# Attention's input normalisation folded into its projection weights; GpSimd's share of a product 160 columns instead of 152; two steps reordered

## The chip, the core and the metric

The kernel runs on one core of one Trainium2 chip. Its time is the device time of one execution in microseconds, taken as the median over several runs. Five engines run at once, each in its own order: TensorE (PE in the profile, its weight loads PEld), VectorE (DVE), ScalarE (ACT), GpSimd (POOL), and SyncE (SP), which here only issues DMAs. They wait for each other through semaphores.

## What is computed

The input x is 8 samples × 512 channels × 2304 positions, in fp32. Two layers are added to it, one after the other, each behind a group norm over 32 groups (mean and variance per group and sample).

```python
x = x + L0(_gn(x), Wq, bq, Wkv, bkv)          # linear attention, 8 heads, causal
x = x + L1(_gn(x), in_proj_w, ...)             # four Mamba blocks in a row

# L0, per sample: q, k, v = three 512x512 projections of the normalised input plus biases
Q, K, V = elu(q) + 1, elu(k) + 1, v
out = causal(Q K^T) V / (Q . cumsum(K) + 1e-10)

# L1, per sample and quarter of 128 channels: u is the quarter plus the output of the one before
xp, z = split(u @ Wi.T); xs = silu(conv(xp)); dt, Bm, Cm = split(xs @ Wx.T)
delta = softplus(dt @ Wdt.T + b)
h[t] = exp(delta[t] * A) * h[t-1] + delta[t] * xs[t] * Bm[t]     # 256 channels x 16 states
y[t] = sum_states(h[t] * Cm[t]) + xs[t] * D;  out = (y * silu(z)) @ Wo.T
```

After each quarter a gated mix (a maximum of input and Mamba output, and two sigmoid weights of means) makes the quarter's output.

## The kernel before

**The Mamba scan is the backbone.** A sample's quarter is cut into 6 chunks of 384 positions. A chunk is a `Job`, and there are 192 of them (8 samples × 4 quarters × 6 chunks). Two `Stream`s alternate, one for even and one for odd samples, by blocks of six jobs; such a block of six is called a pass here. A job has 8 slots, one for each half of the 256 channels and each of four groups of states. In a slot, `slot(k)` emits in this order:

- VectorE: `product` of the next slot (L890, the first 384 − TAIL columns of B × dxr; it reads B from a PSUM copy made by ScalarE at L863), then four `scan`s (L910), each on 128 partitions × 384 positions.
- ScalarE: `decay` (L900), one exponential per scan into a PSUM bank that a scan frees again; at most DEPTH = 3 are ahead (5 in front of the silu and softplus blocks), as far as banks are free.
- GpSimd: `last_product` of the slot after the next (L879, the last TAIL columns of the same product), then `weigh` (L923, the scanned states × C).
- TensorE: `gather` (L937), the sum over states into the bank yp, two slots later.

Besides, at the end of a half `gated` (L949, yz = yp × silu(z)) runs on VectorE, then TensorE projects it (L955) and VectorE takes the maximum (L966, fg). `prepare` makes a job's operands ahead: convolution (L722), gate (L733), silu (L758 to L763), softplus (L793), dx on GpSimd (L834), and the broadcast loads of dr, dxr, B and C through DRAM. `pass_on` mixes a finished quarter into the next one's input: L678 and L684 on TensorE, fu (L682) on ScalarE, xo (L696) on GpSimd, with loads of xb, fu and xo.

**Attention runs beside it.** It has passes too: one (sample, quarter of the output channels o = 0 to 3), six chunks each. `chunk(m)` is a generator; each of its `yield at(j), n` names the half-slot at which its next step is due and how many PSUM banks it needs. Chunks of attention follow each other at 16 half-slots, the length of a job, and lead the Mamba pass that needs them by about 61 half-slots. The steps: project q, k, v (L300, weights `wq` of the pass, biases `bqkv_sb`), features (exp L312 and relu L313 on ScalarE, q L359 and k L367 on VectorE), running sum of k (kc, L373 and L375), v (L378), a kept row (L382), pr = q × kc (L386, VectorE), transposes (L393), denominators and states (L405 to L437), transposes of the broadcast reciprocals (L445), q scaled (L450, VectorE), scores (L457, L467), relu of the scores (L479, ScalarE, `sm`), output (L484 to L498), copy and store (L508), statistics for the second norm (L512).

**Its normalisation.** `statistics(b)` collects mean and variance of a sample's groups (L243, L253), `group_norm` makes `norm`: scale in `norm[:, 0]`, shift in `norm[:, 1]`. In the first pass of each sample (o = 0) a chunk loads x, GpSimd normalises it in place (L324, four instructions of 128 × 384), and the result is stored to DRAM; the other three passes load that stored copy (L275).

**What sets the order.** All engines' programs are written out by hand at build time. `beside(half)` is called twice per slot. It first steps those heads (chunks of attention) whose next step needs no bank, then goes once through the tasks (prepare, pass_on, statistics, finale) and after them the heads, in order, and steps whatever is due and finds its banks free. So a step that needs a bank is emitted behind all tasks of that half-slot, and a step that needs none ahead of them. PSUM: six banks in a list `spare`, taken and returned in the order of emission, so the step that returns a bank determines who waits for whom. DMAs are all issued on SP, in the order of emission; stores wait there at least two half-slots.

Of the kernel before, what the change touches and what calls it, by code (L numbers as in the profile page):

```python
# [9 lines left out]
F32 = mybir.dt.float32  # L10
BF16 = mybir.dt.bfloat16
AF = mybir.ActivationFunctionType
ALU = mybir.AluOpType
# [4 lines left out]
P = 128  # L18
# [1 line left out]
LC = 384  # L20
NI, NQ, NGR = 4, 4, 4
SLOTS = 8
TAIL = 152
BANKS = 6
DEPTH = 3
LEAD = 11
# [23 lines left out]
def attention_then_mamba_kernel(  # L50
# [12 lines left out]
    nc = tc.nc  # L63
    B, _, L = x.shape
    NS = 16
    NC = L // LC
# [30 lines left out]
    wqs = []  # L97
# [72 lines left out]
    def save(out, in_):  # L170
        stores.append((half_no[0], out, in_))
# [48 lines left out]

    norms, xns, x1s, done, ksums = {}, {}, {}, {}, {}

    def statistics(b):

        xv = x[b].rearrange("(t p) l -> p t l", p=P)
        stats = small.tile([P, 4, NC, 6], F32, tag="stats_a", name=f"stats_a{b}", bufs=2)
        if b == 0:

            xs = []

            def load(c):
                t = mpool.tile([P, 4, 1 + LC], F32, tag="u", name=f"xs_{c}", bufs=5)[:, :, 0:LC]
                nc.sync.dma_start(out=t, in_=xv[:, :, c * LC : (c + 1) * LC])
                xs.append(t)

            for c in range(5):
                load(c)
            load_projections()  # L240
            for c in range(NC):
                for ct in range(4):
                    nc.vector.bn_stats(stats[:, ct, c, :], xs[c][:, ct, :])  # L243
                if c == 0:
                    load(5)
                    fetch(0)
        else:
            when = begins[b] + b % 2
            for i in range(4 * NC):
                yield (when - 4, 1) if b > 1 else "1", 0  # L250
                xs = piece(b, i)
                yield (when, 1) if b > 1 else "1", 0
                nc.vector.bn_stats(stats[:, i // NC, i % NC, :], xs)  # L253
                when += PERIOD
        norms[b] = yield from group_norm(stats, 4, f"a{b}", 2)
# [9 lines left out]
    def fetch(m):  # L265

        if m == len(parts):
            return
        b, o, c = parts[m]
        if (o, c) == (0, 0):  # L270
            xns[b] = dpool.tile([512, L], F32, tag="xn", name=f"xn_{b}", bufs=B)
            x1s[b] = dpool.tile([512, L], F32, tag="x1", name=f"x1_{b}", bufs=B)
        xn = apool.tile([P, 4, LC], F32, tag="xn", name=f"xn_{b}_{o}_{c}", bufs=2)
        src = (x[b] if o == 0 else xns[b]).rearrange("(t p) l -> p t l", p=P)
        nc.sync.dma_start(out=xn, in_=src[:, :, c * LC : (c + 1) * LC])  # L275
        fetched[m] = xn

    read, passes = [0], {}

    def chunk(m):  # L280

# [9 lines left out]
        def at(j, gap=1):  # L291
            return times[m] + j, gap
# [4 lines left out]
        def project(j):  # L297
            ps = bank()[:, 0:LC]
            for kt in range(4):
                nc.tensor.matmul(  # L300
                    ps,
                    wqs[m // NC][:, kt, j * P : (j + 1) * P],
                    xn[:, kt, :],
                    start=(kt == 0),
                    stop=(kt == 3),
                )
            return ps, bqkv_sb[:, j * 4 + o : j * 4 + o + 1]

        def feature(ps, bias):

# [2 lines left out]
            nc.scalar.activation(ps, ps, AF.Relu, bias=bias)  # L313
            return ex

        if o == 0:
            yield at(-4), 0
            while b not in norms or m not in fetched:
                yield "1w", 0
            xn, norm = fetched.pop(m), norms[b]  # L320
            for ct in range(4):
                if ct:
                    yield at(ct - 4), 0
                nc.gpsimd.tensor_scalar(  # L324
                    xn[:, ct, :],
                    xn[:, ct, :],
                    norm[:, 0, ct : ct + 1],
                    norm[:, 1, ct : ct + 1],
                    ALU.mult,
                    ALU.add,  # L330
                )
            save(xns[b].rearrange("(t p) l -> p t l", p=P)[:, :, cols], xn)
        while read[0] < m - 1:
            yield "1w", 0
        yield at(0), 1
        if o:
            xn = fetched.pop(m)
        if c == 0:
            passes[b, o] = (
                small.tile([P, 4, 64], F32, tag="S", name=f"S_{b}_{o}", bufs=2),  # L340
# [98 lines left out]
        yield at(15), 0  # L439
        rdb = new("rdb", 1, (P, 2 * NT, 64))  # L440
        nc.scalar.copy(rdb, rd.unsqueeze(2).to_broadcast([P, 2 * NT, 64]))
        yield at(17), 1
        rb = bank()[:, 0:LC].rearrange("p (i t) -> p i t", i=NT)
        for i in range(NT):
            nc.tensor.transpose(  # L445
# [19 lines left out]
        for i in range(NT):  # L465
            for h, sc in zip(heads_of, scs):
# [5 lines left out]
                    stop=i == NT - 1,  # L472
                    skip_group_check=True,
                )
        yield at(20), 0
        sms = []
        for par, sc in enumerate(scs):
            sm = new(f"sm{par}", 1, (P, NT, T))
# [43 lines left out]
    class Stream:  # L522
# [55 lines left out]
        def pass_on(self):  # L578
# [78 lines left out]
            for c in range(NC):  # L657

                cols, icols = slice(c * LC, (c + 1) * LC), slice(3 + c * LC, 3 + (c + 1) * LC)
                if now is None:  # L660
                    first = 2 * self.jobs[self.block * NC + c].start
                    yield (first - 33, 1), 0
                    now = loads(c)
                    yield (first - 25, 1), 0 if old is None else 1
                else:
                    yield "1", 0 if old is None else 1
                fu, xb, xa = now
                now = None
                if not last:
                    normed = dict(bias=norm[:, 1, :], scale=norm[:, 0, :])  # L670
                if old is None:
                    nc.scalar.activation(xi[:, icols], xb, AF.Identity, **normed)
                else:
                    bank = Banks()
                    mixed = bank()[:, 0:LC]
                    more = len(factors) == 3
                    for i, src in enumerate((xi[:, icols], fu)):
                        nc.tensor.matmul(  # L678
                            mixed, mix[:, i, :], src, start=i == 0, stop=i == 1, skip_group_check=True
                        )  # L680
                    yield "1", 0
                    nc.scalar.copy(fu, mixed)  # L682
                    if more:
                        nc.tensor.matmul(  # L684
                            mixed, mix[:, 2, :], xb, start=False, stop=True, skip_group_check=True
                        )
                    yield "1", 0
                    if more:
                        nc.scalar.activation(
                            xi[:, icols], mixed, AF.Identity, bias=norm[:, 1, :]  # L690
                        )
                    elif not last:
                        nc.scalar.activation(xi[:, icols], xb, AF.Identity, **normed)
                    bank.free()
                    self.ready = c + 1
                    nc.gpsimd.tensor_tensor(xa, xa, fu, ALU.add)  # L696
                    save(out[old[0], old[1] * P : (old[1] + 1) * P, cols], xa)
                self.ready = c + 1
                if last and c + 1 < NC:
                    yield "3", 0  # L700
                    now = loads(c + 1)
# [291 lines left out]
    class Task:  # L993
# [16 lines left out]
        def due(self):  # L1010
# [4 lines left out]
                return half_no[0] >= when  # L1015
            return half_no[0] - self.last >= int(when[0])

        def finish(self):
            while self.need is not None:
                self.step()  # L1020
# [22 lines left out]
            yield from job.stream.pass_on()  # L1043


    begun, put, counted = 0, 0, list(range(1, B))
    begins = {}
    for b in counted:
        first = times[parts.index((b, 0, 0))]
# [1 line left out]

    def begin(latest):

        nonlocal begun, put
        while counted and begins[counted[0]] - 4 <= half_no[0]:
            tasks.append(Task(statistics(counted.pop(0))))
        while put < len(parts) and times[put] - 6 <= half_no[0]:
            put += 1
            heads.append(Task(chunk(put - 1), before=heads[-1] if heads else None))
        while (  # L1060
            begun < len(jobs)
            and jobs[begun].start <= latest
            and jobs[begun].stream.block == jobs[begun].block
            and jobs[begun].stream.ready > jobs[begun].c
        ):
            tasks.append(Task(jobs[begun].prepare(), jobs[begun].start))
            begun += 1
# [5 lines left out]
    def beside(half):  # L1073

        half_no[0] = half
        flush(every=False)
        begin(half // 2 + LEAD)

        for t in heads:
            if t.need is not None and t.need[1] == 0 and t.fits() and t.due():  # L1080
                t.step()
        held = False
        for t in tasks + heads:
            while t.need is not None and t.due():
                if not t.fits() or held and t.need[1]:
                    held = held or t.need[1] > len(spare)
                    break
                t.step()
        prune()
# [19 lines left out]
    def at(k):  # L1109
        return jobs[k // SLOTS], k % SLOTS  # L1110
# [198 lines left out]
```

## Time and profile before

| | us |
|---|---|
| runs shown | 8260.18, 8263.85, 8269.36 (median 8263.85) |
| profiled execution, its own time | 8283.94 |
| its span, first to last instruction | 8282.2 |
| before the first scan | 195.1 |
| from there to the last scans | 8060 |
| VectorE busy | 7829.1 |
| GpSimd busy | 7753.9 |
| TensorE busy (granted clock 0.944) | 7354.5 |
| ScalarE busy | 6991.8 |

The profile is of one execution, so durations and waits are of that one. A row of a group reads: line, engine, operation, output <- inputs, shapes, number of instructions | busy time in us, mean of one in ns | idle time of the engine just before them, and what ended it. Each fp32 matmul shows as two matmul instructions with a weight load each. A row of the waits reads: who waited <- for whom: us in total, how often, the longest. In a timeline the bracket holds the idle time before the row and what ended it. "L300" is line 300 of the kernel before. A line with several uses (L910, say) has one row per shape.

### The profile page before, as it was taken

The numbers are of one execution on the slowest core, as the hardware profiler recorded it, in microseconds if no ns is written. First come the engines' busy times: TensorE is split into PE (matmuls) and PEld (weight loads), VectorE is DVE, ScalarE is ACT, GpSimd is POOL, SyncE is SP. The second block draws the span as 40 slices with busy tenths as digits, with TensorE's granted clock in tenths as the row PEclk, the third lists the DMA queues.
The fourth block names the chain that finished last, engine by engine and source line by source line (L and its number), as shares of the span: only waits on it lengthen the run. The fifth ranks groups of instructions, "written<-read, shape, count | busy, mean of one in ns | idle before, by whom it ended". The sixth has DMA issues, their size and how long they took to land. (4 is left out here: it accounts for less than half of the span.)

```text
span 8282.2 us, 133009 instructions
## 1 busy us (share of the span) xinstructions
PE 7354.5 (89%) x39882; PEld 3572.9 (43%) x39882; DVE 7829.1 (95%) x10534; ACT 6991.8 (84%) x14914; POOL 7753.9 (94%) x3905
## 2 busy tenths in 40 slices
PE   8889999998889999998889999999988999998975
PEld 4444444444444444444444444444444444444421
DVE  3999999999999999999999999999999999999998
ACT  3888888888888888888888888888888888888876
POOL 2999999999999999999999999999999999999998
PEclk9999999999999999999999999999999999999976
DMA  6777778777777788777787777877777777777765
GB/s 201 189 189 206 206 200 210 205 196 205 206 200 201 199 210 209 203 205 197 204 213 201 199 206 203 210 207 197 209 204 203 203 201 195 200 200 195 191 170 146
DMA packets 1097348, 1654.99 MB, mean 200 GB/s; under 512 B 143913, under 2 KB 989353, under 8 KB 1096498
## 3 DMA queue, kind: packets, MB, share of 16 engines
q1 hardware_dynamic: 1096626, 1646.48, 76.6%
q8 instruction: 316, 5.18, 0.3%
q14 instruction: 406, 3.33, 0.1%
HBM read 1318.23 MB, written 327.68 MB: 199 GB/s over the span
## 5 line engine op out<-in xcount | busy, mean ns | idle before, releaser
L910 DVE TENSOR_TENSOR_SCAN u<-bank,u 128x385 f32<-128x385 f32 (+1 forms) x6144 | 5447.2, 939 | 115.2 <-ACT bank L900 112.9
L923 POOL TENSOR_TENSOR u<-u,C 128x1536 f32<-128x1536 f32 x1536 | 4894.5, 3187 | 349.1 <-DVE u L910 210.3
L900 ACT ACTIVATE bank<-dr,scales 128x385 f32<-128x385 f32 (+1 forms) x6144 | 3414.1, 579 | 612.8 <-DVE u L910 574.6
L879 POOL TENSOR_TENSOR u<-B,dxr 128x608 f32<-128x608 f32 x1536 | 2286.1, 1488 | 14.5 <-DMA x<-xr 13.8
L300 PE MATMUL bank<-xn,wq 128*128 128x384 f32 x4608 | 1886.5, 558 | 286.1 <-DVE u L910 233.4
L890 DVE TENSOR_TENSOR u<-Bp,dxr 128x928 f32<-128x928 f32 x1536 | 1690.2, 1100 | 10.9 <-ACT Bp L863 7.2
L937 PE MATMUL yp<-u,cst 128*32 128x384 f32 x12288 | 1353.7, 513 | 200.8 <-POOL u L923 122.8
L300 PEld LDWEIGHTS bank<-xn,wq 128*128 128x128 f32 x4608 | 955.4, 216 | 1189.5 <-DVE u L910 373.4
L722 PE MATMUL bank<-xi,wk 128*128 128x384 f32 x3072 | 1102.4, 502 | 7.6 <-ACT xr L508 7.0
L722 PEld LDWEIGHTS bank<-xi,wk 128*128 128x128 f32 x3072 | 555.9, 191 | 561.4 <-DVE u L910 107.7
L937 PEld LDWEIGHTS yp<-u,cst 128*32 128x32 f32 x12288 | 249.1, 109 | 776.7 <-issue 415.7
L900 ACT ACT_TABLE_LOAD x382 | 490.1, 1283 | 6.8
L312 ACT ACTIVATE ex<-bank,bqkv_sb 128x384 f32<-128x384 f32 x384 | 221.4, 577 | 311.5 <-PE bank L300 311.4
L863 ACT COPY Bp<-B 128x464 f32<-128x464 f32 x768 | 420.5, 548 | 21.3 <-DVE u L890 13.1
L834 POOL TENSOR_TENSOR dx<-delta,xs 128x384 f32<-128x384 f32 x384 | 386.0, 1005 | 21.5 <-ACT delta L793 21.5
L678 PE MATMUL bank<-xi,mix 128*128 128x384 f32 x372 | 175.4, 554 | 249.6 <-ACT sm L479 241.4
L955 PE MATMUL bank<-yz,scales 128*128 128x384 f32 x768 | 329.1, 541 | 51.3 <-DVE yz L949 41.7
L782 PE MATMUL bank<-dbc,steps_w 9*128 9x384 f32 x768 | 306.4, 519 | 22.3 <-DVE rd L433 17.6
L733 PE MATMUL bank<-xi,scales 128*128 128x384 f32 x768 | 296.3, 496 | 18.9 <-ACT xs L758 18.8
L769 PE MATMUL bank<-xs,scales 128*40 128x384 f32 x768 | 285.0, 494 | 0.0
L498 PE MATMUL bank<-sm,v 128*64 128x128 f32 x2304 | 254.7, 299 | 0.0
L878 ACT COPY u<-state 128x4 f32<-128x4 f32 x1280 | 249.2, 195 | 0.0
(123 smaller groups left out, 8193.6 us busy)
## 6 DMA issues: line engine op xcount, KB each, us to landing
dr<-dscr SPq DMA_DIRECT2D x1536, 192.0 KB, 4.7
dxr<-xscr SPq DMA_DIRECT2D x1536, 192.0 KB, 5.3
xn<-xn SPq DMA_DIRECT2D x192, 768.0 KB, 5.1
B<-scr SPq DMA_DIRECT2D x1536, 96.0 KB, 4.2
C<-scr SPq DMA_DIRECT2D x1536, 96.0 KB, 2.6
dscr<-delta SPq DMA_DIRECT2D x192, 384.0 KB, 4.8
xscr<-dx SPq DMA_DIRECT2D x192, 384.0 KB, 2.9
xn<-in_x SPq DMA_DIRECT2D x48, 768.0 KB, 5.1
```

What stands on the lines that cost most here:

```text
L300: nc.tensor.matmul(ps, wqs[m // NC][:, kt, j * P : (j + 1) * P], xn[:, kt, :], start=(kt == 0), stop=(kt == 3),)
L722: nc.tensor.matmul(xc, wk[:, k, h * P : (h + 1) * P], xi[:, c0 + k : c0 + k + LC], start=(k == 0), stop=(k == 3),)
L782: nc.tensor.matmul(vp, steps_w[32:41, s, h * P : (h + 1) * P], dbc[32:41, :], start=True, stop=True)
L834: nc.gpsimd.tensor_tensor(dx[:, h, :], delta[:, h, :], xs[:, h, :], ALU.mult)
L863: nc.scalar.copy(self.Bp, self.B[pair % 2][:, :, 0 : LC - TAIL])
L879: nc.gpsimd.tensor_tensor(u[:, :, 1 + LC - TAIL :], self.B[q // 2][:, q % 2, cols].unsqueeze(1).to_broadcast(shape), self.dxr[h][:, :, col ...
L890: nc.vector.tensor_mul(u[:, :, 1 : 1 + LC - TAIL], self.Bp[:, s % 2, :].unsqueeze(1).to_broadcast(shape), self.dxr[s // NQ][:, :, cols],)
L900: nc.scalar.activation(dA[:, cols], self.dr[h][:, g, cols], AF.Exp, scale=w_a[:, self.w[1], NGR * h + g, q : q + 1],)
L910: nc.vector.tensor_tensor_scan(u[:, g, cols], dA[:, cols], u[:, g, cols], 0.0, ALU.mult, ALU.add,)
L923: nc.gpsimd.tensor_tensor(u[:, :, 0:LC], u[:, :, 1:], self.C[q // 2][:, q % 2, :].unsqueeze(1).to_broadcast([P, NGR, LC]), ALU.mult,)
L937: nc.tensor.matmul(self.yp[g * 32 : g * 32 + 32, 0:LC], state_sum, u[:, g, 0:LC], start=False, stop=s % NQ == NQ - 1, skip_group_check=True,)
L955: nc.tensor.matmul(self.xm[:, 0:LC], w_out[:, self.w[1], h, :], self.yz[:, h, :], start=(h == 0), stop=(h == 1),)
```

## The change

Attention's normalised input is no longer made. Scale and shift of a sample's norm go into the weights and biases of each pass instead: a task `adapt` per pass of six chunks computes weights-transposed × shift with 12 small matmuls, adds the biases on VectorE, and scales the four blocks of `wq` on ScalarE in place. All four passes of a sample load x itself; L324 and the store of its result are gone. GpSimd's share TAIL goes from 152 to 160 columns of 384, VectorE's from 232 to 224. The transposes L445, which need a bank, are now stepped in the first loop of `beside`, ahead of the tasks; the relu of the scores (L479), which needs none, no longer is, and so runs behind the tasks. The loads of xb, fu and xo are issued three half-slots later.

```diff
-TAIL = 152
+TAIL = 160
...
-        src = (x[b] if o == 0 else xns[b]).rearrange("(t p) l -> p t l", p=P)
+        src = x[b].rearrange("(t p) l -> p t l", p=P)
...
+    def adapt(i):
+        b, o, _ = parts[i * NC]
+        when = times[i * NC]
+        bank = Banks()
+        yield when - 12, 0
+        while b not in norms or len(wqs) <= i:
+            yield "1w", 0
+        w, norm = wqs[i], norms[b]
+        yield when - 11, 1
+        shift = bank()
+        for j in range(3):
+            for kt in range(4):
+                nc.tensor.matmul(
+                    shift[:, j : j + 1],
+                    w[:, kt, j * P : (j + 1) * P],
+                    norm[:, 1, kt : kt + 1],
+                    start=(kt == 0),
+                    stop=(kt == 3),
+                )
+        yield when - 10, 0
+        bias = small.tile([P, 3], F32, tag="bias", name=f"bias_{i}", bufs=2)
+        nc.vector.tensor_add(
+            bias, shift[:, 0:3], bqkv_sb.rearrange("p (j o) -> p j o", o=4)[:, :, o]
+        )
+        bank.free()
+        for kt in range(4):
+            yield when - 9 + kt, 0
+            nc.scalar.activation(w[:, kt, :], w[:, kt, :], AF.Copy, scale=norm[:, 0, kt : kt + 1])
+        biases[i] = bias
...
-            return ps, bqkv_sb[:, j * 4 + o : j * 4 + o + 1]
+            return ps, biases[m // NC][:, j : j + 1]
...
-        if o == 0:
-            yield at(-4), 0
-            while b not in norms or m not in fetched:
-                yield "1w", 0
-            xn, norm = fetched.pop(m), norms[b]
-            for ct in range(4):
-                if ct:
-                    yield at(ct - 4), 0
-                nc.gpsimd.tensor_scalar(
-                    xn[:, ct, :],
-                    xn[:, ct, :],
-                    norm[:, 0, ct : ct + 1],
-                    norm[:, 1, ct : ct + 1],
-                    ALU.mult,
-                    ALU.add,
-                )
-            save(xns[b].rearrange("(t p) l -> p t l", p=P)[:, :, cols], xn)
+        while m // NC not in biases or m not in fetched:
+            yield "1w", 0
...
-        yield at(17), 1
+        yield at(17), 1, "first"
...
-        yield at(20), 0
+        yield at(20), 0, "late"
...
-                    yield (first - 33, 1), 0
+                    yield (first - 30, 1), 0
...
+        def early(self):
+            return self.need[2] == "first" if len(self.need) > 2 else self.need[1] == 0
...
+        while adapted < 4 * B and times[adapted * NC] - 12 <= half_no[0]:
+            tasks.append(Task(adapt(adapted)))
+            adapted += 1
...
         for t in heads:
-            if t.need is not None and t.need[1] == 0 and t.fits() and t.due():
+            if t.need is not None and t.early() and t.fits() and t.due():
                 t.step()
```

## The prediction

> **What bounds the kernel now.** The first view is the page's busy time with its 40 slices: VectorE 95%, GpSimd 94%, and no stage stands out. With two engines so full, the question is which waits for which, so next come the groups (instruction times) and the waits.
>
> ```profile
> PE 7354.5 (89%) x39882; PEld 3572.9 (43%) x39882; DVE 7829.1 (95%) x10534; ACT 6991.8 (84%) x14914; POOL 7753.9 (94%) x3905
> L923 POOL TENSOR_TENSOR u<-u,C 128x1536 f32<-128x1536 f32 x1536 | 4894.5, 3187 | 349.1 <-DVE u L910 210.3 <-issue 61.7 <-DVE gm_m L191 37.4
> L879 POOL TENSOR_TENSOR u<-B,dxr 128x608 f32<-128x608 f32 x1536 | 2286.1, 1488 | 14.5 <-DMA x<-xr 13.8 <-DMA B<-scr 0.4 <-DMA out<-xo 0.2
> L890 DVE TENSOR_TENSOR u<-Bp,dxr 128x928 f32<-128x928 f32 x1536 | 1690.2, 1100 | 10.9 <-ACT Bp L863 7.2 <-DMA dxr<-xscr 2.7 <-DMA B<-scr 0.8
> L324 POOL TENSOR_SCALAR xn<-xn,norm_a 128x384 f32<-128x384 f32 x192 | 128.8, 673 | 75.6 <-DMA xn<-in_x 61.2 <-PE bank L300 14.0 <-DVE norm_a L211 0.4
> L405 PE MATMUL bank<-cst,pr 128*128 128x2 f32 x1152 | 158.6, 254 | 0.0
> ```
>
> ```profile
> PE bank L678 <- ACT sm L479: 241.4, 173, 1.9
> POOL u L923 <- DVE u L910: 210.3, 151, 2.6
> DVE q L450 <- PE bank L445: 143.2, 129, 4.2
> DVE u L910 <- ACT bank L900: 112.9, 137, 4.8
> ```
>
> GpSimd waits for VectorE's scans, about once per job (a job is a chunk's 8 slots), and scans never wait for GpSimd: VectorE leads. It loses time at two places: at q (L450), which waits for TensorE's transposes, and at a job's last scan, which waits for the decay that ScalarE computes after its silu block. Stretches of two kinds of job follow, cut at the first scan: two ordinary ones, then two in which attention normalises its input (columns: stretch, its us, busy us of PE, PEld, DVE, ACT and POOL with instruction counts, clock, DMA share, GB/s).
>
> ```profile
> 6810.48:6851.42 40.94, 36.82 (x214) 18.04 (x213) 39.65 (x53) 36.53 (x81) 39.53 (x19) 1.00 0.83 214
> 6851.42:6892.36 40.94, 36.82 (x216) 18.13 (x217) 39.65 (x52) 36.53 (x81) 39.53 (x19) 1.00 0.77 198
> 6138.29:6180.42 42.13, 36.33 (x219) 17.72 (x221) 40.28 (x57) 37.05 (x82) 41.92 (x24) 1.00 0.77 201
> 6180.42:6222.61 42.19, 36.69 (x193) 17.42 (x189) 40.05 (x55) 37.05 (x82) 42.19 (x25) 0.96 0.80 217
> ```
>
> Ordinary: VectorE 39.65 plus 1.3 of waits, GpSimd 1.4 free. Normalising: GpSimd has no room left and sets the length. The timeline of TensorE and VectorE in the second ordinary job, just where the change puts its new matmuls:
>
> ```profile
> 6868.18 0.85 PE L937 MATMUL yp<-u,cst 128*32 128x384 f32 x8
> 6869.90 0.91 PE L678 MATMUL bank<-xi,mix 128*128 128x384 f32 x2 [0.87 <-ACT sm L479]
> 6871.30 2.74 PE L300 MATMUL bank<-xn,wq 128*128 128x384 f32 x8
> 6873.88 0.81 PE L684 MATMUL bank<-xb,mix 128*128 128x384 f32 x2
> 6874.52 0.81 PE L373 MATMUL bank<-k,cst 128*128 128x384 f32 x2
> ...
> 6870.71 1.10 DVE L890 TENSOR_TENSOR u<-Bp,dxr 128x928 f32<-128x928 f32 x1
> 6871.72 3.50 DVE L910 TENSOR_TENSOR_SCAN u<-bank,u 128x385 f32<-128x385 f32 x4
> ```
>
> TensorE is behind: its kc matmul (L373) of this slot starts when three of the slot's four scans are done.
>
> **The change part by part.** The sum is made against the profiled execution, 8283.94 us (8282.2 span); the median of the runs is 8263.85, 0.24% below, and I apply the difference to the median.
>
> *Share of 160 columns.* L890 loses 32 elements. Slope between L949 (384 elements, 551 ns) and L890 (928, 1100): 1.01 ns, so 32 ns × 1536 = −50 us. Two of a job's eight products stand between the scan that lets ScalarE go and the scan that waits for it; there the wait grows by what they save: 164 such jobs × 65 ns = 11 back. Net −39. GpSimd's L879 gains 32: 59 ns by the slope from L879 to L923, 69 from L834 (384 elements, 1005 ns) to L879, 78 by L879's own ratio. I take 69, the nearest pair: +106 us, 0.55 per job. The 192 normalisations take 129 away. Ordinary jobs: GpSimd 39.53 → 40.1, VectorE 39.65 − 0.26 plus 0.9 of decay wait = 40.3. GpSimd stays hidden by 0.2; I charge 0.1 per job for so little room (+18) and +6 in the last two passes, where attention is over and GpSimd leads: +24. If the cover is gone, see rival three.
>
> *Normalisation gone.* 48 of 192 chunks lose four L324 (2.67 us) and one 768 KB store each; SP has 48 issues fewer. In the 38 jobs that hold them after the start, GpSimd's lateness shows as late transposes; what of those L450 waits the next item doesn't take is 23 us: −20.
>
> *Transposes first.* In the program's order L445 now stands ahead of L955 in 183 jobs. L955 waits for yz and takes 0.8 us, so L445 was behind both. The gaps before L450 after the scans begin add up to 134 us in 125 jobs. But fg (L966) needs L955 and stands two VectorE operations (0.53 + 0.55) behind L450: only the first 1.0 us of each gap can go, the rest moves to L966. Gap by gap that is −95.
>
> *Relu later.* Its bank no longer comes to L678, which takes the bank that k (L367) frees. TensorE starts this stretch about 0.8 us earlier, and L300 behind it finds the relu done. That removes pr's wait (L386, 16 us after the start), most of yz's (L949, 13) and ScalarE's for the gate (L763, 17, passed on to the last scan): −46.
>
> *The adaptation, once per pass, 32 times.* 24 matmul instructions (12 fp32 pairs, N = 1), a bias add on VectorE, four ScalarE scalings. L405 has the same weights and N = 2: six start to start take 0.69 us, 0.83 with the end; so 2.8 to 3.3, and I take 2.9. In the built order they take L373's place in slot 4, and the bias add stands after that slot's second scan. In the job above: L678 at 6869.1, hence the burst where L373 stood less 0.8, 6873.7, done 6876.6. VectorE has its second scan done at 6873.3. So VectorE stands still for 3.3 us in front of a 0.15 us add (row: L191 on four columns), and scans, then GpSimd, queue behind it. kc now follows the output matmuls: 6876.6 + gather 0.8 + L484 to L498 3.05 + kc 1.4 + copy 0.5 = 6882.35; pr stands 4.55 us of VectorE work behind the add, at 6881.35: 1.0 more. Together 4.45 × 30 passes amid scans = +134. Bounds: 0 (if TensorE is there 3 us earlier) and 8 (below). The scalings (0.55 each as L313 on as many elements, +70 us of ScalarE, −10 from the shorter L863) fall into gaps that this standstill leaves: nothing; uncovered, 0.8 × 30 = 24.
>
> *Loads three half-slots later.* xb, fu, xo move on SP past the dxr, dr and scr issues. fu lands 2.6 us after issue (at most 6.1) and came 14 us early; 6 remain: nothing. Uncovered, 2 us in few jobs.
>
> *Start.* 195 us before the first scan. Each of the next five chunks loses 2.6 us of GpSimd between load and projection (−13); the first gains about 7 (burst and scalings in a row): −6.
>
> Sum: −39 + 24 − 20 − 95 − 46 + 134 − 6 = **−48 us**; 8263.85 − 48 = **8216**.
>
> *Clock.* In the job at 7143.22 the granted clock is 0.92:
>
> ```profile
> 7148.91 5.49 PE L300 MATMUL bank<-xn,wq 128*128 128x384 f32 x8 [1.37 <-DVE u L910]
> 7154.19 1.91 PE L955 MATMUL bank<-yz,scales 128*128 128x384 f32 x4
> ```
>
> The eight L300 took 5.49 us against 2.74 above, after waits of 0.65 and 1.37: this half clock makes the long L450 waits. [...]
>
> **The rivals.**
> 1. *The burst is hidden.* For it: TensorE's 4 us free per job. Against it: they lie elsewhere, the stretch up to slot 4 is packed. −48 − 134 = −182: 8082. Chance 0.12.
> 2. *The burst costs more than it brings (slower).* In slot 4 of each pass the clock falls to half during or after it; two windows of half clock (6.8 us) lose 3.4 us of TensorE work, which VectorE waits out at bias and pr: 7.85 instead of 4.45, +102, 8318. It decides from 6.05 per pass (4.45 + 48/30). For it: the half clock in the job above. Against it: L405 bursts ran at full clock. 0.16.
> 3. *GpSimd becomes the bound.* With 78 ns per L879 and the 0.3 us that a normalising job has over GpSimd's busy time, ordinary jobs take 0.3 more, in some 150 jobs: +45, 8261, no change. Against it: 1.4 us free now. 0.14.
> 4. *The reorder doesn't do what it says*: L300 ahead of L445, at half clock, keeps the q wait as it is: +95, 8311. 0.06.
>
> **How the numbers follow.** The forecast has 0.52. About 0.2% (17 us) is what a measurement of this kernel can tell from no change, so faster is below 8247, slower above 8280. Faster: 0.47 of the forecast, 0.12 of rival one, 0.05 of three: 0.64. Same: 0.03 + 0.02 (two) + 0.08 + 0.01 (four) = 0.14. Slower: 0.02 + 0.14 + 0.01 + 0.05 = 0.22. Range: from 8110 (most of the burst hidden) to 8325 (rivals two and four in).
>
> **What would show it.** Right: L890 near 1068 ns, L879 near 1557; L324 gone and normalising jobs as long as the others; L450's wait near 20 to 40, some of it at L966; L678's wait for the relu gone; a new wait of about 100 us of the bias add for its bank, 3.3 each, and about 1.0 at pr; ordinary jobs 40.4, the adapting one 45. Wrong: the bias add waits under 1 us (rival one); half clock in slot 4 (two); POOL's wait for scans below 40 us in total (three); L450 still over 100 (four).

## The result and the profile after

The changed kernel takes 8309.02 us (median of 4 runs, 8304.91 to 8314.4) against 8266.6 us for the kernel before on the same chip (8260.18 to 8276.44): a ratio of 1.0051 (95% interval 1.0033 to 1.0068). It is slower by 0.5%, where 0.6% faster was forecast. The profiled execution took 8314.4 us, its span 8312.6, at a granted clock of 0.934.

Most of what was forecast is there all the same. First the page, busy times and groups (from mid-chunk on, a line of the changed kernel is 14 higher than in the kernel before: L890 is L904, L879 is L893, L923 is L937):

```profile
PE 7523.5 (91%) x40650; PEld 3679.9 (44%) x40650; DVE 7778.3 (94%) x10566; ACT 7025.7 (85%) x15042; POOL 7730.8 (93%) x3713
L937 POOL TENSOR_TENSOR u<-u,C 128x1536 f32<-128x1536 f32 x1536 | 4890.2, 3184 | 370.7 <-DVE u L924 288.6
L893 POOL TENSOR_TENSOR u<-B,dxr 128x640 f32<-128x640 f32 x1536 | 2387.4, 1554 | 12.6 <-DMA B<-scr 12.6
L904 DVE TENSOR_TENSOR u<-Bp,dxr 128x896 f32<-128x896 f32 x1536 | 1631.4, 1062 | 11.6 <-DMA dxr<-xscr 11.6
```

VectorE has 51 us less work and the kernel is 30 us longer in this view, so what is new is waiting. The view of waits (total, times, longest) names it:

```profile
DVE u L924 <- ACT bank L914: 177.2, 177, 4.2
DVE bias L301 <- PE bank L292: 88.9, 32, 4.5
DVE pr L400 <- ACT before L396: 53.3, 27, 5.5
DVE q L464 <- PE bank L459: 36.5, 66, 4.2
PEld bank L692 <- DVE k L381: 139.2, 173, 1.9
PE bank L692 <- DVE k L381: 16.8, 41, 1.2
POOL u L937 <- DVE u L924: 288.6, 209, 5.9
```

The q wait fell from 143.2 to 36.5, and L692 now waits for k in place of the relu, its matmuls for 16.8 us where L678's waited 241.4: the reorder did what it says. The bias add's wait was forecast at about 100. Not forecast is the first row: scans wait 64 us longer for ScalarE's decays than before (112.9). The stretches of an ordinary job and of the adapting job behind it (columns as in the windows before):

```profile
7087.40:7127.60 40.20, 36.96 (x214) 17.84 (x213) 39.23 (x52) 36.39 (x81) 39.97 (x19) 1.00 0.82 219
7127.60:7175.50 47.90, 43.76 (x239) 23.29 (x240) 39.84 (x53) 38.46 (x85) 40.30 (x20) 0.89 0.68 169
```

The ordinary job is 40.2 us (40.94 before, 40.4 forecast). The adapting one is 47.9, not 45. Its timeline, reduced to the rows that hand the delay on:

```profile
7150.77 2.73 PE L292 MATMUL bank<-norm_a,wq 128*128 128x1 f32 x24
7153.55 0.16 DVE L301 TENSOR_TENSOR bias<-bank,bqkv_sb 128x3 f32<-128x3 f32 x1 [3.03 <-PE bank L292]
7154.61 0.58 ACT L914 ACTIVATE bank<-dr,scales 128x385 f32<-128x385 f32 x1 [2.31 <-DVE u L924]
7158.02 0.81 PE L389 MATMUL bank<-before,cst 128*128 128x384 f32 x2
7158.86 0.47 ACT L396 COPY before<-bank 64x384 f32<-64x384 f32 x1 [2.33 <-PE bank L389]
7159.36 0.62 ACT L307 ACTIVATE wq<-wq,norm_a 128x384 f32<-128x384 f32 x1
7159.37 0.56 DVE L400 TENSOR_TENSOR pr<-q,bank 128x384 f32<-128x384 f32 x1 [1.25 <-ACT before L396]
7161.58 0.62 ACT L307 ACTIVATE wq<-wq,norm_a 128x384 f32<-128x384 f32 x1
7163.85 0.63 ACT L307 ACTIVATE wq<-wq,norm_a 128x384 f32<-128x384 f32 x1
7164.82 0.59 ACT L882 ACTIVATE yp<-xs,scales 128x384 f32<-128x384 f32 x1
7165.56 0.85 PE L951 MATMUL yp<-u,cst 128*32 128x384 f32 x8 [2.51 <-ACT yp L882]
7166.34 4.54 PE L736 MATMUL bank<-xi,wk 128*128 128x384 f32 x8
7166.53 0.62 ACT L307 ACTIVATE wq<-wq,norm_a 128x384 f32<-128x384 f32 x1
7170.92 0.58 ACT L775 ACTIVATE xs<-bank,scales 128x384 f32<-128x384 f32 x1 [0.89 <-PE bank L736]
7174.63 1.81 DVE L924 TENSOR_TENSOR_SCAN u<-bank,u 128x385 f32<-128x385 f32 x2 [2.72 <-ACT bank L914]
```

Down to pr this is the forecast: bias add 3.03 (3.3 forecast), pr 1.25 (1.0). Then come the scalings (L307), which had been costed at nothing. ScalarE's copy L396 has waited 2.33 us for kc, which stands behind the burst. From there up to 7170.03 ScalarE does not pause: eleven microseconds, 2.5 of them scalings, three of the four ahead of L882. So L882 (the product with D, which opens the next half's accumulation) is late, TensorE stands 2.51 us in front of gather L951, and drops to half clock: this convolution takes 4.54 us, the one at 7159.54 took 2.85. Now the silu block waits for it (0.89), the decay behind the block is late, and the last scan waits 2.72 us where 0.93 is usual.

### The profile page after: what moved, and what is told of

It is laid out like the page before. It is cut to its first block, busy times and chain, and to the rows that moved or that the text cites. A ratio compares the mean times of both kernels' runs of the same rounds, so it can differ in the third digit from the quotient of the medians.

```text
span 8312.6 us, 134855 instructions
## 1 busy us (share of the span) xinstructions
PE 7523.5 (91%) x40650; PEld 3679.9 (44%) x40650; DVE 7778.3 (94%) x10566; ACT 7025.7 (85%) x15042; POOL 7730.8 (93%) x3713
## 4 chain that ended last, share of the span: by engine, by line
DVE 32%; PE 28%; ACT 19%; DMA 9%; issue 7%; POOL 3%; SPq 2%; ACTq 0%; DVEq 0%; POOLq 0%
DVE u L924 23%; PE bank L330 11%; ACT bank L914 7%; DVE u L904 5%; PE bank L736 3%; ACT L914 3%; PE yp L951 3%; DMA dxr<-xscr 2%; POOL u L937 2%; PE bank L747 2%; DMA dr<-dscr 1%; ACT L772 1%; PE bank L692 1%; PE bank L969 1%; DMA dscr<-delta 1%
## 5 line engine op out<-in xcount | busy, mean ns | idle before, releaser
L924 DVE TENSOR_TENSOR_SCAN u<-bank,u 128x385 f32<-128x385 f32 (+1 forms) x6144 | 5446.8, 935 | 177.8 <-ACT bank L914 177.2
L937 POOL TENSOR_TENSOR u<-u,C 128x1536 f32<-128x1536 f32 x1536 | 4890.2, 3184 | 370.7 <-DVE u L924 288.6
L893 POOL TENSOR_TENSOR u<-B,dxr 128x640 f32<-128x640 f32 x1536 | 2387.4, 1554 | 12.6 <-DMA B<-scr 12.6
L951 PE MATMUL yp<-u,cst 128*32 128x384 f32 x12288 | 1360.9, 515 | 323.9 <-ACT yp L882 175.6
L904 DVE TENSOR_TENSOR u<-Bp,dxr 128x896 f32<-128x896 f32 x1536 | 1631.4, 1062 | 11.6 <-DMA dxr<-xscr 11.6
L736 PE MATMUL bank<-xi,wk 128*128 128x384 f32 x3072 | 1144.0, 517 | 11.0 <-ACT xr L522 10.6
L736 PEld LDWEIGHTS bank<-xi,wk 128*128 128x128 f32 x3072 | 577.1, 198 | 588.8 <-DVE u L924 114.0
L951 PEld LDWEIGHTS yp<-u,cst 128*32 128x32 f32 x12288 | 250.4, 109 | 952.6 <-POOL u L937 457.0
L342 ACT ACTIVATE ex<-bank,bias 128x384 f32<-128x384 f32 x384 | 221.2, 576 | 339.5 <-PE bank L330 339.2
L877 ACT COPY Bp<-B 128x448 f32<-128x448 f32 x768 | 409.2, 533 | 24.7 <-DMA B<-scr 16.3
L747 PE MATMUL bank<-xi,scales 128*128 128x384 f32 x768 | 313.3, 506 | 42.4 <-ACT xs L772 42.4
```

Of the source, the lines that this page charges most:

```text
L736: nc.tensor.matmul(xc, wk[:, k, h * P : (h + 1) * P], xi[:, c0 + k : c0 + k + LC], start=(k == 0), stop=(k == 3),)
L747: nc.tensor.matmul(zp, w_gate[:, s, h * P : (h + 1) * P], xi[:, c0 + 3 : c0 + 3 + LC], start=True, stop=True,)
L877: nc.scalar.copy(self.Bp, self.B[pair % 2][:, :, 0 : LC - TAIL])
L893: nc.gpsimd.tensor_tensor(u[:, :, 1 + LC - TAIL :], self.B[q // 2][:, q % 2, cols].unsqueeze(1).to_broadcast(shape), self.dxr[h][:, :, col ...
L904: nc.vector.tensor_mul(u[:, :, 1 : 1 + LC - TAIL], self.Bp[:, s % 2, :].unsqueeze(1).to_broadcast(shape), self.dxr[s // NQ][:, :, cols],)
L924: nc.vector.tensor_tensor_scan(u[:, g, cols], dA[:, cols], u[:, g, cols], 0.0, ALU.mult, ALU.add,)
```

## The experiments

The theory from this trace: the failed term is the adaptation, and in it the scalings. The rivals: reorder or share brought less than thought; the burst alone does all of it through the clock. Line numbers in the rows are those of each experiment's own kernel; the operations' names tell which is meant. c0 to c5 are the six jobs of a pass; the change adapts in c2. e1, e2, e3 and e12 leave parts of the adaptation out, and e12 doubles one, so they tell prices only; the others compute the whole. Times of different runs are subtracted as they stand. The kernel before, measured again beside each, had medians from 8266.6 to 8276.19 us, so such a difference is uncertain by some 10 us.

### Leaving the adaptation out, whole and in parts

e1: shift, bias add and scalings left out for passes 1 to 31.

```diff
-        (shift matmuls, bias add)          # kept for i == 0
+        bias = bqkv_sb.rearrange("p (j o) -> p j o", o=4)[:, :, o]
...
-            nc.scalar.activation(w[:, kt, :], w[:, kt, :], AF.Copy, scale=norm[:, 0, kt : kt + 1])
+            if i == 0: (the same)
```

> Leaves out the shift matmuls, the bias add and the four weight scalings of passes 1 to 31 (so those passes run on unnormalised input); the first pass keeps them. Theory: the adaptation is the whole miss. A c2 job of a pass is 47.9 us with it and was 41.2 without it in the last block (job 182), and the job after it is some 0.5 to 1 us long, so 31 x 6.7 to 7.7 = 208 to 239 us go: 8070 to 8101, and every job 40.2 to 41.7. Rival: the reorder or the share cost what is lost and the adaptation costs only the forecast 4.45 x 31 = 138 or less: 8171 or more.

Measured: 8101.28 us, ratio 0.9789 (0.9773 to 0.9805). The adaptation costs 8309.02 − 8101.28 = 208 us, 6.7 per pass (by the two ratios 217, or 7.0, as the kernel before took 8274.88 beside e1), and the rest of the change is worth 174, where the forecast without its adaptation term was 182. The job that adapted is 41.1 us:

```profile
6934.07:6975.19 41.12, 39.49 (x216) 19.49 (x217) 39.48 (x53) 36.45 (x81) 40.16 (x20) 0.92 0.81 201
```

e2: only the four scalings left out.

```diff
-            nc.scalar.activation(w[:, kt, :], w[:, kt, :], AF.Copy, scale=norm[:, 0, kt : kt + 1])
+            if i == 0: (the same)
```

> Leaves out only the four weight scalings on ScalarE of passes 1 to 31 (weights stay unscaled there). Theory: the scalings, costed at nothing, push the product with D (L882) late, TensorE then stands 2.5 us before gather L951, drops to half clock and the silu block comes late: 3.2 us of the 7.7 per pass are theirs, the c2 job falls from 47.9 to some 44.7 and the time to 8309 - 31 x 3.2 = 8210 (8185 to 8235). Rival (the forecast's term for them, 0 to 0.8 per pass): the burst alone sets off the half clock, 8285 to 8309.

e3: only shift matmuls and bias add left out (`bias` is the raw one, as in e1).

> Keeps the four scalings and leaves out the twelve shift matmuls and the bias add of passes 1 to 31 (the raw bias is used). Theory: what stays is the scalings' own delay of ScalarE, 2 to 3 us per pass, c2 job 43 to 44.5, time 8070 to 8101 plus 31 x 2 to 3 = 8135 to 8190. Rival: scalings hurt only because the burst has already made TensorE late, then within 15 us of the run without any adaptation.

Measured: e2 8231.62 (0.9945; 0.993 to 0.996), e3 8120.12 (0.981; 0.9796 to 0.9825). Over the 8101.28 of neither:

| | us | per pass |
|---|---|---|
| scalings alone (e3) | +19 | 0.6 |
| burst and bias add alone (e2) | +130 | 4.2 |
| both (the change) | +208 | 6.7 |

Burst and bias add cost what was forecast (4.45). The scalings cost 2.5 per pass beside them (2.8 by the ratios), 0.6 without, where nothing was forecast. In e2 the waits of bias add and pr are those of the change; only the decay row is back at e1's (116.9):

```profile
DVE u L925 <- ACT bank L915: 117.9, 141, 4.0
DVE bias L301 <- PE bank L292: 89.0, 32, 4.5
DVE pr L401 <- ACT before L397: 54.7, 27, 5.5
```

So the 59 us by which L924 waits longer in the changed kernel are the scalings' doing. With 14 us at q's factor (L464, 36.5 for 22.6) and 8 at fg (15.6 for 7.7), these waits make up the whole of what the scalings cost there. e3's expected 2 to 3 per pass was wrong: alone they still fit.

### Why the two cost more together

e12: no burst and no bias add, each scaling done twice.

```diff
+            if i:
+                nc.scalar.activation(w[:, kt, :], w[:, kt, :], AF.Copy, scale=norm[:, 0, kt : kt + 1])
```

> As e3 (no shift matmuls and no bias add in passes 1 to 31), but each of the four scalings is done twice in a row, 1.24 us in place of 0.62 in each of four half slots. It tells why the scalings cost 0.6 us per pass alone and 2.5 beside the burst. Theory: ScalarE has 1.7 us of idle time in those half slots (slots 4 to 5.5 of an ordinary job in the trace after: 1.06, 0.18, 0.37 and 0.15); what goes beyond it is paid about whole, whoever uses it up (four more scalings here, the wait of 2.33 for k's prefix sum beside the burst), so 2 to 2.5 us per pass more than e3: 8120 + 62 to 78 = 8180 to 8200. Rival: the extra cost needs the burst (TensorE late, then at half clock), and eight scalings cost twice what four do: 8135 to 8145.

Measured: 8212.42 (0.9931; 0.9916 to 0.9945). The second four scalings cost 92 us, 3.0 per pass (100 and 3.2 by the ratios); the first four cost 0.6. No burst is needed: ScalarE's idle time runs out. The adapting job shows the same chain with nothing but scalings ahead of it:

```profile
7074.79 0.57 ACT L888 ACTIVATE yp<-xs,scales 128x384 f32<-128x384 f32 x1
7075.51 1.00 PE L957 MATMUL yp<-u,cst 128*32 128x384 f32 x8 [2.02 <-ACT yp L888]
7076.44 4.35 PE L742 MATMUL bank<-xi,wk 128*128 128x384 f32 x8
7084.53 0.96 DVE L930 TENSOR_TENSOR_SCAN u<-bank,u 128x385 f32<-128x385 f32 x1 [2.67 <-ACT bank L920]
```

Late product with D, TensorE idle for 2.02 us, a convolution at half clock (4.35), a last scan 2.67 late. The price per added microsecond is above one (3.0 for 2.5 of work); the half clock that follows the idle time is one visible reason: the clock falls 34 to 36 us into 23 of the 30 adapting jobs of e12, in e3 into none. Its share was not measured by itself. An estimate from the traces bounds it: TensorE spent 1059.5 us at half clock in e12 and 954.3 in e3, and lost at most half of the 105 between, 53 of the 92 us; between e2 (980.8) and the change (1097.0) it is at most 58 of the 78.

e13: the whole adaptation one half slot later, so that the burst stands behind kc on TensorE and pr ahead of the bias add on VectorE.

```diff
-        yield when - 11, 1
+        yield when - 10, 1
...
-        yield when - 10, 0
+        yield when - 9, 0
...
-            yield when - 9 + kt, 0
+            yield when - 8 + kt, 0
```

> The changed kernel with the whole adaptation one half slot later (shift at slot 4.5, bias add at 5, scalings at 5.5 to 7): TensorE's burst now stands behind k's prefix matmul, and the product pr ahead of the bias add on VectorE. Theory (pr and ScalarE's copy of the sums stand behind the burst, which is 1.25 us of VectorE per pass and sends ScalarE into the scalings 2.33 us late): the bias add's wait of 3 stays, pr's goes, and of the 2.5 of the scalings half or more: 31 x 2 to 3.5 = 62 to 108 less, 8200 to 8247. Rival: the outputs behind the burst and scalings nearer to the silu block cost as much, 8290 or more.

Measured: 8232.23 (0.9955; 0.9938 to 0.9971), 77 us less than the change.

```profile
DVE u L924 <- ACT bank L914: 136.3, 149, 4.2
DVE yz L963 <- PE yp L951: 75.5, 29, 6.3
DVE bias L301 <- PE bank L292: 61.5, 32, 4.5
DVE pr L400 <- ACT before L396: 17.1, 6, 4.2
```

pr's wait is back at what e1 has (17.1), decays are 41 us better and the bias add's wait 27, and yz pays 68 of it back. It waits for the gather at the half's end, which stands behind burst and outputs, and in 27 of the 30 adapting jobs (9 in the change) the clock falls to half behind the burst, so that four output matmuls take 0.69 us for 0.44. That pr and the decays recover supports the order around kc as the cause of ScalarE's lateness.

e5: only the bias add moved, behind the second scaling.

```diff
-        yield when - 10, 0
-        (bias add)
...
+            if kt == 1: (bias add)
```

> The changed kernel with one edit: the bias add is issued two half slots later (behind the second scaling instead of ahead of the first). Theory A: VectorE's 3.03 us standstill is a matter of place, it goes whole: 31 x 3.0 = 93 us, some 8215, c2 job 44.9. Rival B: the 2.73 us of matmuls lie on a TensorE that is full there, so the wait comes back at the next reader of TensorE (the product pr, L400, or the fourth scan's decay); then 8280 or more, c2 job 47 or more.

Measured: 8276.37 (1.0002; 0.9993 to 1.0011). Of the 93 us expected 33 came. The bias add's row is gone, and in its place

```profile
DVE pr L400 <- ACT before L396: 61.3, 28, 4.2
DVE k L381 <- ACT bank L343: 38.7, 21, 6.6
DVE yz L963 <- PE yp L951: 36.9, 32, 6.4
DVE pr L400 <- PE bank L389: 13.7, 7, 2.5
```

stand at 53.3, 21.6, 7.0 and (after the first scan) 6.8 in the change. Neither theory alone holds: where TensorE is full, an early reader's wait moves for the larger part to the next readers.

### The other terms of the sum

e6: the kernel before with the new order of L445 and L479 alone.

```diff
-        yield at(17), 1
+        yield at(17), 1, "first"
...
-        yield at(20), 0
+        yield at(20), 0, "late"
```

> The kernel before with nothing but the new order of two steps: the transposes behind q's last factor (L445) first, the scores' relu late; share 152, normalisation and loads as before. The forecast's terms: transposes first -95, relu later -46, together -141: 8125 (8090 to 8170), VectorE's wait before L450 from 143 to some 35 us. Rival: the wait only moves on to the next reader of TensorE (fg, L966) or to the last scan's decay, 8230 or more.

Measured: 8171.19 (0.9877; 0.9862 to 0.9892): −101 where −141 stood.

```profile
DVE q L450 <- PE bank L445: 46.2, 58, 5.9
DVE fg L966 <- PE bank L955: 20.0, 32, 2.2
```

L450's wait fell by 97, but 18 of it moved to fg (2.2 before), which leaves 79 of the transposes' 95. Of the relu's 46, some 28 came: after the first scan pr's wait fell from 16.1 to 1.9, yz's from 18.0 to 9.0 and the decays' by 5, while ScalarE's for the gate rose (16.9 to 24.1).

e7: the kernel before with `TAIL = 160` alone.

> The kernel before with 160 columns of each product on GpSimd instead of 152, nothing else. The forecast's terms: L890 -50 of which 11 come back at the decays, and +24 for jobs in which GpSimd has little room: -15 in all, but with the normalisation still on GpSimd in 8 passes (11.0 us a pass measured more busy there) up to +20: 8225 to 8285. Rival: GpSimd becomes the bound: 8300 or more.

Measured: 8276.98 (1.0002; 0.9993 to 1.0012): nothing. Added up from the trace after the first scan, L450's wait grew from 134 to 154 us. In all, VectorE's work fell by 46 us and its idle time grew by 35: it came to the same waits earlier.

### Other places for the adaptation

e4: weights fetched two chunks earlier, shift in two parts at slot 0.5, scalings spread.

```diff
+        for js, go, add in (([0, 1], when - 49, when - 47), ([2], when - 33, when - 31)):
+            yield go, 1
+            shift = burst(js)
+            yield add, 0
...
+        for kt, go in enumerate((when - 30, when - 27, when - 14, when - 11)):
```

> Complete computation. The projection weights of the next pass are fetched two chunks earlier; the shift is cut in two (eight and four matmuls) at slots 0.5 of two jobs, where the trace after shows TensorE idle 0.5 to 1.0 us in slots 0 to 1; each bias add stands two half slots behind its matmuls; the four scalings go one each to slots 2.5 and 4 of two jobs, where ScalarE is idle 0.9 and 1.1 us. Theory (the place is what costs): 0 to 1.5 us per pass are left, 8075 to 8145, faster than before by 1.5 to 2.3%. Rival (the work itself costs, TensorE has 3 us of idle per job at most and the burst is 2.73): 2.7 to 4 per pass, 8155 to 8220.

Measured: 8383.73 (1.0129; 1.0113 to 1.0145), far outside both expectations. The trace of its first shifting job:

```profile
7117.22 3.57 PE L295 MATMUL bank<-norm_a,wq 128*128 128x1 f32 x16 [3.42 <-ACT delta L813]
7120.73 1.50 PE L957 MATMUL yp<-u,cst 128*32 128x384 f32 x8
7122.16 4.55 PE L336 MATMUL bank<-xn,wq 128*128 128x384 f32 x8
```

The idle time of TensorE that was to be used was itself a wait for a bank, and the burst takes a bank too: it waits 3.42 us for softplus (L813) to give one back, with the gather and the projection queued behind it, and then all run at half clock (1.50 for 0.85). The c0 job became 49.5 us. Its c2 job, with two scalings at slots 2.5 and 4, is 40.2: there they cost nothing.

e11: burst and bias add as in the change, one job earlier; scalings spread.

```diff
-        yield when - 11, 1
+        yield when - 27, 1
...
-        for kt in range(4):
-            yield when - 9 + kt, 0
+        for kt, go in enumerate((when - 22, when - 14, when - 11, when - 6)):
+            yield go, 0
```

> The changed kernel with the burst and its bias add as they are (slot 4, the add one half slot behind), but one job earlier, and the four scalings spread to slots 6.5 of that job and 2.5, 4 and 6.5 of the next, where ScalarE stands idle 0.4 to 1.1 us; the weights are fetched one chunk earlier. Theory: what the scalings cost beside the burst (8309 against 8232 without them, 2.5 us per pass; 0.6 per pass alone) is their place behind the late product pr, and goes: 8225 to 8245. Rival: any scaling that has to stand in ScalarE's order costs it, 8270 or more.

Measured: 8253.61 (0.998; 0.997 to 0.9989), 55 us less than the change and 22 more than e2, between the two expectations. The job with three scalings is 40.2 us; the one with the burst 45.1 in the median, and 49.7 in the one shown in the last section.

e8: four matmuls each behind kc in chunks 2, 3 and 4, into a spare column of v's bank; bias by ScalarE.

```diff
+        if carried:
+            shifted(i, j, vbank[:, LC : LC + 1])      # 4 matmuls
...
+            nc.scalar.activation(
+                bias[:, j : j + 1], vbank[:, LC : LC + 1], AF.Identity, bias=raw(i, j)
+            )
...
+        for kt, go in enumerate((when - 22, when - 14, when - 11, when - 6)):
```

> Complete computation. The next pass's weights are fetched three chunks earlier; its shift is cut in three pieces of four matmuls, one behind k's prefix matmul of each of the chunks 2, 3 and 4, into a spare column of the bank that the v projection already holds (no bank of its own); the piece's bias add is a 128x1 ScalarE copy with bias behind vT's (nothing on VectorE); the four scalings go one each to slots 6.5, 2.5, 4 and 6.5 of the two jobs after. Theory (place and bank are what costs, 0.9 us of matmuls at a time find room): the run without adaptation plus 0 to 1 us per pass, 8095 to 8135. Rival (TensorE is full and its 2.73 us are paid wherever they lie): 8101 + 85 = 8185 or more.

Measured: 8146.77 (0.9846; 0.9831 to 0.986): 45 us over e1, 17 of them in the start (215.4 for 198.0). pr waited again (35.8 of the 60.1 after the first scan), for the copy that now stood behind a later vT:

```profile
DVE pr L428 <- ACT before L424: 60.1, 52, 9.8
```

e9: that copy ahead of vT, and the second pass's adaptation later.

```diff
+        if ksum is not None: (copy and store of kc's sums)
         vT = new("vT")
...
-        yield when - 26, 0
+        yield when - (26 if i > 1 else 13), 0
```

> The carried version with two edits: ScalarE copies the prefix sums out (L396 of the changed kernel) ahead of vT instead of behind it, since vT now waits for the piece of shift in its bank and the product pr waited 35.9 us in all for that copy; and the second pass's adaptation stands 13 half slots ahead, not 26, since the start grew from 198.0 to 215.4 us. Theory: 31 x 1.1 us and some 8 us of start go, 8147 - 42 = 8105 (8095 to 8125), 1.8 to 2.1% faster than before. Rival (ScalarE's wait for the piece only moves to the next decay): 8135 or more.

Measured: 8137.2 (0.9838; 0.9824 to 0.9853), 10 less than e8 and not 42: the rival's side. pr's row fell to 17.0, the decays' rose from 123.4 to 136.8, and the start hardly moved (212.8).

e10: e9 with `TAIL = 152`.

> The same kernel as e9 with 152 columns on GpSimd instead of 160: the share by itself, where GpSimd no longer normalises. The forecast's term: L890 50 us longer on VectorE, 11 of them hidden at the decays, so 39 us slower than e9, some 8145. Rival (e7 measured nothing for the share alone): TensorE and ScalarE set the jobs, then within 12 us of e9.

Measured: 8148.41 (0.9853; 0.9836 to 0.9869). 11 us for the share: every run of e10 is above every run of e9, but the intervals of the ratios overlap, so between nothing and about 25; not 39.

e14: four matmuls in chunk 1, eight in chunk 3, fetch in chunk 0 (in the first pass in chunk 4).

```diff
+        i, js = m // NC + 1, {1: [0], 3: [1, 2]}.get(c, [])
```

> Complete computation. As e9, with the pieces of the shift in other chunks: four matmuls in chunk 1 and eight in chunk 3 (jobs c4 and c0, 41.1 to 41.2 us in e9 whether they carry a piece or not) instead of four each in chunks 2, 3 and 4 (c5 and c1 were 40.96 with a piece and 40.21 without); weights fetched in chunk 0, in the first pass in chunk 4 as in the changed kernel (the fetch in chunk 1 put 768 KB ahead of the first loads of x: the start was 212.8 us). Theory: 31 x 1.5 and some 7 us of start less than e9, not below the run without adaptation: 8105 to 8120. Rival: eight matmuls in one place cost c0 what c5 and c1 gain, 8130 or more.

Measured: 8162.14 (0.9872; 0.9857 to 0.9886), slower than e9. The jobs with eight matmuls are 42.3 us in the median (41.1 in e9), as the rival said; the start fell to 204.1.

e15: e9 with the changed kernel's fetch and adaptation in the first two passes.

```diff
-        if c == NC - 5:
+        if c == (NC - 2 if m < NC else NC - 5):
             load_projections()
```

> Complete computation: e9 (three pieces of four matmuls behind k's prefix matmul in chunks 2, 3 and 4) with the start of the changed kernel: the first pass fetches the next weights in chunk 4 and the second pass's adaptation stands where the changed kernel has it. Theory: the start falls from 212.8 to 204 us as in e14 and the scans stay at 7896, so 8128 (8120 to 8135), 1.6 to 1.8% faster than before. Rival (the weights' fetch is not what lengthened the start): 8137 again.

Measured: 8131.36 (0.9824; 0.981 to 0.9837), as expected, with a start of 207.9. This is the fastest complete version here, 1.8% faster than the kernel before. Of the 30 us to e1, 10 are the start; most of the rest goes with the pieces: the jobs that carry those of chunks 2 and 4 take 40.96 us, 40.21 in e1, and c0 and c2 give back 1.05 of these 1.5 per pass.

## Why the prediction was wrong

**The step that failed is the adaptation's**, and in it the sentence that the scalings "fall into gaps that this standstill leaves: nothing". The standstill did leave ScalarE a gap (2.31 us in front of the decay at 7154.61). But the scalings overwrite weights that the burst reads, and in ScalarE's order they stand behind that gap and behind the copy that waits 2.33 us for kc; after it no gap was left. Measured beside the burst they cost 2.5 us per pass; the "uncovered" price of 0.8 was too low as well. The other part, 4.45 for bias add and pr, measured 4.2 (e2). Together 6.7, above the point of 6.05 that the text gave for slower.

**Rival two was on the right side for another reason**, and that its 8318 lies within 9 us is luck. The text has it from 6.8 us of half clock in slot 4 of each pass, which the change does not show. Counted in its trace, the clock falls between 22 and 31 us into 9 of the 30 adapting jobs after the first scan, where the burst stands (for 3.41 us in eight of them, for 10.24 in one), and between 36 and 41.5 us into 27 of them, where ScalarE's lateness does it; without the scalings (e2) it is 9 and none. In the kernel before, around the text's row at 7148.91, the clock was at half from 7148.28 to 7155.11, 6.83 us; of the waits of 0.65 and 1.37 only 1.4 us in all lie ahead of the fall.

**The rest of the sum was right in total (−182 against −174 in e1), less so by term.** e6 gave −101 for transposes and relu, where −141 stood. By the waits the transposes brought 79 of 95, since fg took back 18 of the 97 won at L450; of the relu's 46, pr's 16 and yz's 13 were largely found, the gate's 17 not. Share: −39 + 24 forecast, 0 in e7 and 11 in e10. Normalisation gone: −20 forecast; e1 − e6 is −70, and with 0 to 11 off for the share −59 to −70 are left for it and the later loads. It was not run by itself. The passes around a sample's first fell most, as the eighth, from 261.3 us (e6) to 247.8 (e1).

**Start:** forecast −6, measured 195.1 to 205.8. e1, which keeps the first pass's adaptation, starts at 198.0, so 8 of the 11 us are the second pass's, which falls into the start too and was left out of the count.

**Right:** L904 1062 ns (1068), L893 1554 (1557), GpSimd never the bound (288.6 us of waiting for scans), ordinary jobs 40.2 (40.4), L464 36.5 with 15.6 at fg, bias add 88.9 (about 100).

## What to carry to other kernels

An operation put on a nearly full engine must be priced with the engine's idle time in those very slots, after every other delay of the same change has been placed; two additions that each fit may not fit together (0.6 and 4.2 us per pass apart, 6.7 together), so sum them per engine and slot before calling either free. Idle time in front of an instruction is room only for work that doesn't need what that instruction waits for, here a PSUM bank (in e4 the burst itself waited 3.42 us for one). Small pieces carried by steps that already hold a bank, and scalings put where ScalarE is seen idle, turned the same change from 0.5% slower into 1.8% faster.

## What the runs showed of the hardware

TensorE's clock fell without TensorE standing still. In e11, around a burst of 24 one-column matmuls (windows; the column before the DMA share is the granted clock), and its timeline:

```profile
7046.00:7054.50 8.50, 8.33 (x42) 4.62 (x41) 8.31 (x10) 6.04 (x15) 8.50 (x6) 1.00 0.32 100
7054.50:7057.60 3.10, 3.10 (x28) 3.02 (x26) 0.00 (x0) 1.59 (x5) 3.10 (x3) 0.87 1.11 217
7057.60:7066.00 8.40, 8.40 (x38) 3.50 (x38) 4.57 (x6) 1.67 (x3) 5.58 (x3) 0.50 0.70 146
...
7054.57 3.08 PE L292 MATMUL bank<-norm_a,wq 128*128 128x1 f32 x24
7057.58 1.50 PE L951 MATMUL yp<-u,cst 128*32 128x384 f32 x8
7059.02 1.65 PE L498 MATMUL bank<-xr,cst 128*128 128x384 f32 x2
```

TensorE is busy 3.10 of 3.10 us, nearly all of it (3.02) with weight loads that have one column behind each, and the clock is at 0.50 right after it: L951 takes 1.50 for 0.85, L498 1.65 for 0.91. By the mean of 0.87 in the middle row the clock fell at about 7056.8; TensorE's last wait ahead of that, 0.17 us, ended at 7049.95. This doesn't follow every burst: after the first scan it is 9 of 30 in the change, 15 in e11, 27 in e13.

In the traces of the kernel before and of the change the profiler's record of the clock changes only at steps of 3.41 us: half clock lasted 3.41 us 59 times in the change, 6.83 us 96 times, and longer 14 times. In the change, what goes with the fall behind a burst is how the burst lies among these steps. Nine of the 30 bursts have 2.19 to 2.74 us within one step, and in all nine half clock begins where that step ends; the other 21 have at most 2.10 us within one step, and none of them is followed by it there. What exactly the clock counts isn't shown. The change's later fall, at 7166.47 in the job above, comes behind 2.51 us of waiting (7163.05 to 7165.56); in e12 the waiting is 2.02.
